# First convolution by halves of the images, its norm finished in two parts, parameters prepared beside it

## The chip, the cores and the metric

The kernel runs on one core of one Trainium2 chip. The time is that of the whole program on the device, in microseconds (us); lower is better. TensorE is called PE, VectorE DVE, ScalarE ACT, GpSimd POOL and SyncE SP, as in the profile.

## The reference

Two layers work on 32 images of 96 channels, 56 x 56 points, all in float32:

```python
# layer 0
h = conv7x7_per_channel(x) + conv_b
h = (h - mean_over_channels(h)) * rsqrt(var_over_channels(h) + 1e-5) * ln_g + ln_b
h = gelu(h @ w1 + b1)          # 96 -> 384, at each point
h = (h @ w2 + b2) * layer_scale
x = h + x
# layer 1
x = silu(conv5x5_per_channel(x) + conv_b)
dts, Bs, Cs = split(x_proj_w @ x)
delta = softplus(dt_w @ dts + dt_b)
P = exp(cumsum(max(delta * A, log(1e-9))))
hs = P * cumsum(delta * Bs * x / max(P, 1e-9))
y = sum_n(hs * Cs) + x * Ds
```

The mean and the variance at a point go over all 96 channels, so the first convolution must be done for every channel before a point can be normalised.

## The kernel before

The program has four stages, each with its own pools in SBUF: the first convolution, the MLP, the second convolution, and the scan. Between them everything goes through DRAM.

**Preparation.** SP loads all parameters (L105 to L131) and then the two sets of convolution kernels. DVE spreads the 7 x 7 kernels into zeroed rows (`pad`, L150 to L156), SP stores them as `taps1_d`, and from there they come back as Toeplitz matrices. In between stand the 5 x 5 kernels (`taps2_d`) and the MLP's and the scan's weights: folded with the norm's gain and the layer scale by small matmuls (L182, L190, L207) and copied into place by DVE.

**First convolution.** The 32 images lie as two halves of 16 (`j`), 56 image rows each, so 112 rows of 896 points for a channel. For each of the 96 channels SP loads the Toeplitz matrix `wt` (two DMAs from `taps1_d`, in `toeplitz`, three buffers) and the two image halves `xt`; DVE, POOL and ACT copy even and odd columns into `xq` (three zeroed buffers); PE does four taps by two halves (L286), both with the same weights one after the other; ACT adds the bias into `ht` (L294); POOL's queue stores `ht` to `conv1_d` (L298). DVE and ACT keep running sums of the difference to channel 0 and of its square (`acc1`, `acc2`, L302 to L305). After the last channel the norm is finished for all points (L308 to L316): square, subtract, Sqrt on ACT, reciprocal on DVE, and a store to `rstd_d`.

**MLP.** 28 groups of four rows. `load_rows(n)` loads `r` (the norm, repeated over 32 partitions), three tiles `h` of `conv1_d` and three tiles `x` of four DMAs each, two groups ahead. `normalise` multiplies `h` by `r` on DVE; `hidden` does the first matmul (L372, PSUM tiles `ph`, three buffers) and Gelu on ACT (L382); `result` the second (L391, `po`) and the sum with `x` into `o` (L402); POOL's queue stores `o` to `block_d`. A group has two parts `k`, each of three steps in which PE does `hidden` and then `result` of the part before. Groups 0 to 13 hold the rows of half `j = 0`, groups 14 to 27 those of `j = 1`.

**Order.** Instructions marked `pin` keep the order of the text on their engine. The others, those of the first convolution and all loads of the MLP among them, are placed by the compiler's scheduler, which may move them far ahead if buffers and data allow. A DMA on SP's or ACT's queue also waits for one of eight semaphore lanes, that is for the DMA that had this lane before it. Tiles in DRAM are followed by region: a load waits for the stores that write what it reads.

Of the kernel before, what the change touches and what calls it, by code (L numbers as in the profile page):

```python
# [8 lines left out]
F32 = mybir.dt.float32  # L9
# [37 lines left out]
def convnext_then_scan_kernel(  # L47
# [38 lines left out]
    def column(src, n, name):  # L86
        t = const.tile([n, 1], F32, name=name)
        nc.sync.dma_start(t, src.rearrange("(p o) -> p o", o=1))
        return t

    def across(src, parts, n, name):
        t = const.tile([parts, n], F32, name=name)
        nc.sync.dma_start(t, src.rearrange("(o n) -> o n", o=1).to_broadcast([parts, n]))
        return t
# [9 lines left out]

    c1b_t = across(c1b, ROWS, C, "c1b_t")  # L105
    c2b_t = across(c2b, 128, C, "c2b_t")
    g_t = column(ln_g, C, "g_t")
    lnb_t = column(ln_b, C, "lnb_t")
    b2_t = column(b2, C, "b2_t")
    ls_t = column(ls, C, "ls_t")  # L110
    ls_b = across(ls, 128, C, "ls_b")
    dtb_t = column(dtb, C, "dtb_t")
    ds_t = column(ds, C, "ds_t")
    w1_t = const.tile([C, F], F32, name="w1_t")
    nc.sync.dma_start(w1_t, w1)
    b1_t = const.tile([128, 3], F32, name="b1_t")
    nc.sync.dma_start(b1_t, b1.rearrange("(f p) -> p f", p=128))
    w2_t = const.tile([128, 3, C], F32, name="w2_t")
    nc.sync.dma_start(w2_t, w2.rearrange("(f p) c -> p f c", p=128))
    xp_t = const.tile([R, C], F32, name="xp_t")  # L120
    nc.sync.dma_start(xp_t, xp[:R, :])
    xpT_t = const.tile([C, R + 2 * N], F32, name="xpT_t")
    nc.sync.dma_start(xpT_t, xpT)
    dtwT_t = const.tile([R, C], F32, name="dtwT_t")
    nc.sync.dma_start(dtwT_t, dtwT)
    a_t = const.tile([128, NG], F32, name="a_t")
    for g in range(NG):
        nc.sync.dma_start(
            a_t[:, g : g + 1],
            bass.AP(alog.tensor, alog.offset + g * DG, [[1, DG], [C, N], [1, 1]]),  # L130
        )  # L131

    w1r_t = const.tile([128, C // CB, F], F32, name="w1r_t")
    b1p_t = const.tile([128, 3], F32, name="b1p_t")
    b2r_t = const.tile([128, C // CB], F32, name="b2r_t")
    wd_t = const.tile([C, C], F32, name="wd_t")
# [4 lines left out]

    with tc.tile_pool(name="prep", bufs=1) as prep, tc.tile_pool(
        name="prep_ps", bufs=1, space=PSUM
    ) as prep_ps:


        kt = prep.tile([C, K1, K1], F32, name="kt1")
        nc.sync.dma_start(kt, c1w.rearrange("c (i j) -> c i j", j=K1))
        pad = prep.tile([C, 3, WP, P1], F32, name="pad1")
        nc.vector.memset(pad, 0.0)  # L150
        at = H - 1 - K1 // 2
        for i in range(3):
            for t in range(P1):
                j = 2 * t + 1 - i
                if j in range(K1):
                    nc.vector.tensor_copy(pad[:, i, at : at + K1, t], kt[:, :, j])  # L156
        nc.sync.dma_start(taps1_d, pad.rearrange("c d p t -> c (d p t)"))

        kt = prep.tile([C, K2, K2], F32, name="kt2")
        nc.sync.dma_start(kt, c2w.rearrange("c (i j) -> c i j", j=K2))  # L160
        turned = prep.tile([C, K2, K2], F32, name="turned")
        for r in range(K2):
            nc.vector.tensor_copy(turned[:, r], kt[:, K2 - 1 - r])
        pad = prep.tile([C, QC, 2 * RW, QC * 2], F32, name="pad2")
        nc.vector.memset(pad, 0.0)
        for k in range(QC):
            for f in range(QC):
                for t in range(2):
                    j = 4 * t + (k if k < 2 else k - 4) - f + K2 // 2
                    if j in range(K2):  # L170
                        nc.vector.tensor_copy(
                            pad[:, k, RW - K2 : RW, f * 2 + t], turned[:, :, j]
                        )
        nc.sync.dma_start(taps2_d, pad)


        cen = prep.tile([C, C], F32, name="cen")
        nc.vector.tensor_scalar(cen, ident[:C, :C], -1.0 / C, None, ALU.add)
        w1g = prep.tile([C, F], F32, name="w1g")
        nc.vector.tensor_scalar(w1g, w1_t, g_t, None, ALU.mult)  # L180
        ps = prep_ps.tile([C, 512], F32, name="ps_w1")
        nc.tensor.matmul(ps[:, :F], lhsT=cen, rhs=w1g, start=True, stop=True)  # L182
        for i in range(RB):
            for d in range(C // CB):
                nc.vector.tensor_copy(
                    w1r_t[CB * i : CB * i + CB, d, :], ps[CB * d : CB * d + CB, :F]
                )
        ps = prep_ps.tile([128, 512], F32, name="ps_b1")
        for f in range(3):
            nc.tensor.matmul(  # L190
                ps[:, f : f + 1], lhsT=w1_t[:, f * 128 : (f + 1) * 128], rhs=lnb_t,
                start=True, stop=True,
            )
        nc.vector.tensor_add(b1p_t, ps[:, :3], b1_t)

        for f in range(3):
            nc.vector.tensor_mul(w2_t[:, f, :], w2_t[:, f, :], ls_b)
        b2p_t = prep.tile([C, 1], F32, name="b2p_t")
        nc.vector.tensor_mul(b2p_t, b2_t, ls_t)
        for i in range(RB):  # L200
            for d in range(C // CB):
                nc.vector.tensor_copy(
                    b2r_t[CB * i : CB * i + CB, d : d + 1], b2p_t[CB * d : CB * d + CB]
                )

        ps = prep_ps.tile([C, 512], F32, name="ps_wd")
        nc.tensor.matmul(ps[:, :C], lhsT=xp_t, rhs=dtwT_t, start=True, stop=True)  # L207
        nc.vector.tensor_copy(wd_t, ps[:, :C])


        nc.vector.memset(bcw_t, 0.0)
        nc.vector.tensor_copy(bcw_t[:, : 2 * N], xpT_t[:, R:])
        nc.vector.memset(pick_t, 0.0)
        for k in range(4):
            rows = slice(32 * k, 32 * k + 2 * N)
            at = 32 * k + (k // 2) * N
            nc.vector.tensor_copy(
                pick_t[rows].rearrange("p (d n) -> p d n", n=N),
                ident[rows, at : at + N].rearrange("p (o n) -> p o n", o=1).to_broadcast(
                    [2 * N, DG, N]  # L220
                ),
            )
        nc.vector.tensor_reduce(
            sel_t, ident.rearrange("p (d n) -> p d n", n=N), mybir.AxisListType.X, ALU.add
        )
        nc.vector.tensor_scalar(dsm_t, ident[:C, :C], ds_t, None, ALU.mult)
        nc.scalar.activation(a_t, a_t, AF.Exp)
        nc.vector.tensor_scalar(a_t, a_t, -1.0, None, ALU.mult)

    def toeplitz(taps_d, wt, k, c, m):

        n = (k + 1) // 2
        for s in range(2):
            taps = bass.AP(
                taps_d.tensor, taps_d.offset + (c * 3 + 1 - s) * WP * n,
                [[n, H], [WP * n, 2], [1, m * n]],  # L240
            )
            nc.sync.dma_start(wt[MP * s : MP * s + H], taps)
        return wt.rearrange("p o m -> p (o m)").rearrange("p (q t) -> p t q", t=n)
# [4 lines left out]
    def two(t):  # L248
        return t.rearrange("p (s q) -> p s q", s=2)

    with tc.tile_pool(name="c1", bufs=3) as pool, tc.tile_pool(
        name="c1k", bufs=1
    ) as keep, tc.tile_pool(name="c1_ps", bufs=4, space=PSUM) as psum:
        wts = [keep.tile([128, 2, H * P1], F32, name=f"wt1_{i}") for i in range(3)]
        xqs = [keep.tile([128, B2, BI, W2 + 3], F32, name=f"xq_{i}") for i in range(3)]
        for t in wts + xqs:
            nc.vector.memset(t, 0.0)
        first = keep.tile([ROWS, COLS], F32, name="first")
        acc1 = keep.tile([ROWS, COLS], F32, name="acc1")
        acc2 = keep.tile([ROWS, COLS], F32, name="acc2")  # L260
        nc.vector.memset(acc1, 0.0)
        nc.vector.memset(acc2, 0.0)

        def by_row(d, s):

            return d[:, s * PQ : (s + 1) * PQ].rearrange("(j m) q -> m j q", j=B2)

        for c in range(C):
            wv = toeplitz(taps1_d, wts[c % 3], K1, c, H)
            xt = pool.tile([128, COLS], F32, name=f"xt1_{c}", tag="xt")  # L270
            for j in range(B2):
                nc.sync.dma_start(xt[MP * j : MP * j + H], x[c, j * H : (j + 1) * H])
# [24 lines left out]
            for s in range(2):  # L297
                nc.gpsimd.dma_start(by_row(conv1_d[c], s), two(ht)[s * H : (s + 1) * H])  # L298
# [502 lines left out]
```

## Time and profile before

| | |
|---|---|
| time, median of 3 runs | 3668.39 us (3664.61 to 3669.38) |
| profiled execution: time, span | 3661.97 us, 3660.2 us |
| first matmul of the first convolution | 27.68 us |
| one channel of it, steady | 6.03 us |
| ACT takes up its last channel | 608.99 us |
| first matmul of the MLP | 642.85 us |
| first matmul of the second convolution | 1505.63 us |
| PE, DVE, ACT, POOL busy | 83%, 73%, 64%, 53% |
| DMA share, 100 to 500 us and 640 to 1500 us | mostly 0.4 to 0.6 |

The page's slices are 91.5 us each: the first convolution fills slices 1 to 7, the MLP 8 to 16, the second convolution about 17 to 20, the scan the rest. A digit is the busy share in tenths. In a timeline line the first two numbers are start and length, and the bracket gives the idle time before it and what ended that. A group's line has busy time and mean of one in ns, and after the last bar the idle time before its instructions.

### The profile page before, as it was taken

The numbers are of one execution on the slowest core, as the hardware profiler recorded it, in microseconds if no ns is written. First come the engines' busy times: TensorE is split into PE (matmuls) and PEld (weight loads), VectorE is DVE, ScalarE is ACT, GpSimd is POOL, SyncE is SP. The second block draws the span as 40 slices with busy tenths as digits, with TensorE's granted clock in tenths as the row PEclk, the third lists the DMA queues.
The fourth block names the chain that finished last, engine by engine and source line by source line (L and its number), as shares of the span: only waits on it lengthen the run. The fifth ranks groups of instructions, "written<-read, shape, count | busy, mean of one in ns | idle before, by whom it ended". The sixth has DMA issues, their size and how long they took to land. (4 is left out here: it accounts for less than half of the span.)

```text
span 3660.2 us, 46554 instructions
## 1 busy us (share of the span) xinstructions
PE 3054.0 (83%) x17290; PEld 1284.6 (35%) x17290; DVE 2670.0 (73%) x1867; ACT 2343.2 (64%) x2133; POOL 1951.4 (53%) x1241
## 2 busy tenths in 40 slices
PE   7999996899999999899948777777777777777775
PEld 5777774333333333334312222222222222222221
DVE  5666665233333333699949999999999999999998
ACT  3555553333333333588858888888888888888884
POOL 2333331122222222100038998898898898898896
PEclk9999998899999999999966666667667667667666
DMA  5555553455555554699977877877877877877873
GB/s 153 167 167 169 168 166 108 150 162 162 160 163 160 162 158 121 183 285 292 289 235 251 276 245 272 275 258 262 272 250 266 277 256 262 278 253 265 278 256 109
DMA packets 302055, 790.70 MB, mean 216 GB/s; under 512 B 123012, under 2 KB 180164, under 8 KB 277156
## 3 DMA queue, kind: packets, MB, share of 16 engines
q1 hardware_dynamic: 259076, 669.31, 56.6%
q0 software_dynamic: 28416, 79.87, 7.2%
q10 hardware_dynamic: 14336, 38.54, 2.8%
q8 instruction: 137, 2.24, 0.3%
q14 instruction: 90, 0.74, 0.1%
HBM read 551.83 MB, written 235.74 MB: 215 GB/s over the span
## 5 line engine op out<-in xcount | busy, mean ns | idle before, releaser
L681 POOL TENSOR_TENSOR hs<-hs,ct 128x1568 f32<-128x1568 f32 x192 | 672.9, 3505 | 102.8 <-DVE hs L670 91.0
L654 POOL TENSOR_TENSOR rep<-rep,bt 128x1568 f32<-128x1568 f32 x192 | 674.5, 3513 | 14.5 <-DMA rep<-du_d 14.5
L382 ACT ACTIVATE g<-ph,b1p_t 128x896 f32<-128x896 f32 x336 | 320.1, 1004 | 512.2 <-PE ph L372 512.2
L402 DVE SCALAR_TENSOR_TENSOR o<-po,b2r_t,x 128x224 f32<-128x224 f32 x336 | 190.5, 609 | 572.3 <-PE po L391 572.3
L286 PE MATMUL ps<-xq,wt 120*112 120x448 f32 x1536 | 581.2, 539 | 14.4 <-POOL xq L281 14.4
L414 POOL DMA_DIRECT2D block_d<-o x336 | 183.0, 552 | 703.8 <-DVE o L402 621.8
L286 PEld LDWEIGHTS ps<-xq,wt 120*112 120x112 f32 x1536 | 429.4, 280 | 165.9 <-POOL xq L281 14.6
L372 PE MATMUL ph<-h,w1r_t 32*128 32x448 f32 x4032 | 440.1, 559 | 55.7 <-DVE h L362 54.0
L599 POOL TENSOR_TENSOR du<-du,xs 96x784 f32<-96x784 f32 x128 | 236.2, 1846 | 367.1 <-ACT du L593 367.1
L585 PE MATMUL pz<-xs,wd_t 96*96 96x392 f32 x512 | 268.6, 688 | 182.6 <-ACT du L593 147.9
L391 PE MATMUL po<-g,w_t 128*32 128x448 f32 x4032 | 413.1, 543 | 0.0
L694 PE MATMUL py<-hs,sel_t 128*32 128x392 f32 x1536 | 330.0, 680 | 85.5 <-POOL hs L681 85.5
L661 DVE TENSOR_TENSOR_SCAN pv<-rep,pv 128x1568 f32<-128x1568 f32 x96 | 329.1, 3428 | 59.9 <-DMA rep<-du_d 43.3
L666 DVE SCALAR_TENSOR_TENSOR pv<-pv,rep 128x1568 f32<-128x1568 f32 x192 | 345.6, 1800 | 21.1 <-POOL hs L681 1.4
L630 PE MATMUL pk<-bn,pick_t 8*128 8x392 f32 x1024 | 284.9, 672 | 87.2 <-ACT y L704 68.1
L661 DVE TENSOR_TENSOR_SCAN pv<-rep,carry_p,pv 128x1568 f32<-128x1568 f32 x96 | 334.9, 3489 | 9.5 <-DVE hs L670 0.5
L670 DVE TENSOR_TENSOR_SCAN hs<-rep,carry_h,pv 128x1568 f32<-128x1568 f32 x96 | 334.1, 3480 | 10.0
L480 PE MATMUL ps<-xq,wt 128*32 128x448 f32 x3072 | 308.4, 547 | 34.2 <-DMA xq<-block_d 31.8
L670 DVE TENSOR_TENSOR_SCAN hs<-rep,pv 128x1568 f32<-128x1568 f32 x96 | 328.4, 3420 | 9.9 <-PE pk L630 0.5
L503 DVE COPY st<-yt 28x896 f32<-28x896 f32 x288 | 317.6, 1103 | 20.6 <-ACT yt L494 8.5
L687 PE MATMUL py<-xs,dsm_t 96*96 96x392 f32 x512 | 318.9, 768 | 14.5 <-ACT bn L618 9.5
L648 ACT ACTIVATE rep<-rep,a_t 128x1568 f32<-128x1568 f32 x192 | 308.4, 1606 | 12.5 <-DMA rep<-du_d 12.2
(87 smaller groups left out, 3473.1 us busy)
## 6 DMA issues: line engine op xcount, KB each, us to landing
rep<-du_d SPq DMA_DIRECT2D x192, 1568.0 KB
du_d<-du SPq DMA_DIRECT2D x128, 588.0 KB
xq<-block_d SPq DMA_DIRECT2D x192, 225.0 KB
block_d<-o POOLq DMA_DIRECT2D x336, 120.0 KB, 5.6
xt<-in_x_dram SPq DMA_DIRECT2D x192, 196.0 KB
h<-conv_d SPq DMA_DIRECT2D x84, 448.0 KB
x<-in_x_dram SPq DMA_DIRECT2D x336, 112.0 KB
conv_d<-st SPq DMA_DIRECT2D x96, 392.0 KB
```

The costliest lines, as they stand in the source:

```text
L286: nc.tensor.matmul(ps[:, j, :PQ].rearrange("p (i r) -> p i r", i=BI), lhsT=wv[:KR, t], rhs=xq[:KR, j, :, t : t + W2], start=(t == 0), stop ...
L372: pin(nc.tensor.matmul(phs[i // 2][:, i % 2, :HALF], lhsT=w1r_t[rows, d, f * 128 : (f + 1) * 128], rhs=hts[n, d][rows, s * HALF : (s + 1) ...
L382: nc.scalar.activation(gt, ph[:, :, :HALF], AF.Gelu, bias=b1p_t[:, f : f + 1], scale=1.0)
L391: pin(nc.tensor.matmul(po[CB * i : CB * i + CB, :HALF], lhsT=w2_t[:, f, CB * d : CB * d + CB], rhs=gts[n, s, f, i // 2][:, i % 2], start=( ...
L503: pin(copy(st[:, :, :, :, f], yt[RW * f : RW * f + QR].rearrange("p h (b q) -> p h b q", q=QW),))
L654: pin(nc.gpsimd.tensor_mul(ut, ut, bts[i // NG]))
L661: pin(nc.vector.tensor_tensor_scan(run, da, zero, carry_p[:, col : col + 1] if q else 1.0 / EPS, ALU.mult, ALU.add))
L666: pin(nc.vector.scalar_tensor_tensor(run, in0=run, scalar=1.0, in1=ut, op0=ALU.min, op1=ALU.mult))
L670: pin(nc.vector.tensor_tensor_scan(ht, da, run, carry_h[:, col : col + 1] if q else 0.0, ALU.mult, ALU.add))
L681: pin(nc.gpsimd.tensor_mul(ht, ht, cts[k]))
L687: pin(nc.tensor.matmul(half(py[:C], s), lhsT=dsm_t, rhs=tokens(k, 2 * h + s, 4), start=True, stop=False,))
L694: pin(nc.tensor.matmul(py[g * DG : (g + 1) * DG, s, :BK], lhsT=sel_t, rhs=hss[k * NG + g][:, cols], start=False, stop=True, tile_position= ...
```

## The change

The convolution's loop goes over 192 halves `n` instead of 96 channels: first all channels of `j = 0`, then all of `j = 1`, so the taps of a channel are loaded twice. The sums are kept for each half apart. `finish_norm(0)` stands two halves into the second 96, `finish_norm(1)` in the MLP at `k == 3`. The convolution's pools stay open through the MLP, which gets fewer buffers for `x` and `g`. SP loads the 7 x 7 kernels and three image halves first; the other parameters go on ACT's queue, and what prepares them is split into pieces (`beside`) of which one follows each half from the seventh on. Some memsets move from DVE to POOL.

```diff
+    def finish_norm(j):
+        acc1, acc2 = acc1s[j], acc2s[j]
+        sq = keep.tile([ROWS, HALF], F32, name=f"sq_{j}")
+        nc.vector.tensor_mul(sq, acc1, acc1)
...
+        nc.scalar.activation(acc2, acc2, AF.Sqrt, bias=eps_t[:ROWS], scale=1.0)
+        nc.vector.reciprocal(acc1, acc2)
+        for s in range(2):
+            nc.gpsimd.dma_start(
+                rstd_d[j * H : (j + 1) * H, s * PQ : (s + 1) * PQ], acc1[s * H : (s + 1) * H]
+            )
...
+        name="c1_ps", bufs=8, space=PSUM
...
+        kt1 = prep.tile([C, K1, K1], F32, name="kt1")
+        nc.sync.dma_start(kt1, c1w.rearrange("c (i j) -> c i j", j=K1))
+        def load_x(n):
+            j, c = divmod(n, C)
+            xts[n] = pool.tile([H, COLS], F32, name=f"xt1_{n}", tag="xt", bufs=4)
+            nc.sync.dma_start(xts[n], x[c, j * H : (j + 1) * H])
+        for n in range(3):
+            load_x(n)
...
+            nc.scalar.dma_start(t, src.rearrange("(p o) -> p o", o=1))
...
+        beside = [first_weights] + [lambda i=i: first_rows(i) for i in range(RB)]
+        beside += [second_weights, scan_weights, scan_rows, turn_taps]
+        beside += [lambda k=k: second_taps(k) for k in range(QC)]
+        def taps_of(n):
+            c, wt = n % C, wts[n % len(wts)]
+            for s in range(2):
...
+                nc.sync.dma_start(wt[MP * s : MP * s + H], taps)
+        for n in range(2):
+            taps_of(n)
+        for n in range(B2 * C):
+            j, c = divmod(n, C)
+            if n + 2 < B2 * C:
+                taps_of(n + 2)
+            if n + 3 < B2 * C:
+                load_x(n + 3)
+            xq = xqs[n % len(xqs)]
+            xv = xts.pop(n).rearrange("p (i r s) -> p s i r", i=BI, s=2)
+            copy = nc.vector.tensor_copy if n % 2 else nc.gpsimd.tensor_copy
+            copy(xq[:H, :, 2 : W2 + 2], xv[:, 1])
+            nc.scalar.copy(xq[MP:KR, :, 1 : W2 + 1], xv[:, 0])
...
+            for t in range(P1):
+                nc.tensor.matmul(ps..., lhsT=wv[:KR, t], rhs=xq[:KR, :, t : t + W2], ...)
...
+            if n >= 6 and beside:
+                beside.pop(0)()
+            if n == C + 2:
+                finish_norm(0)
...
-            nc.vector.memset(t, 0.0)
+            nc.gpsimd.memset(t, 0.0)
...
-                xt = pool.tile([128, COLS], F32, name=f"x_{n}_{d}", tag="x", bufs=9)
+                xt = pool.tile([128, COLS], F32, name=f"x_{n}_{d}", tag="x", bufs=6)
...
-                gt = pool.tile(..., name=f"g_{n}_{s}_{f}_{a}", tag="g", bufs=15)
+                gt = pool.tile(..., name=f"g_{n}_{s}_{f}_{a}", tag="g", bufs=14)
...
+            if k == 3:
+                finish_norm(1)
```

The buffers: `wt` three, for two halves ahead and the one in use; `xq` four; `xt` four; PSUM eight single banks. As the scheduler has built it, SP's queue in the convolution holds for each half two tap loads and one image load, and between them the MLP's first loads: 24 DMAs of `x` (groups 0 and 1), `h` of group 0 behind the taps of halves 35, 71 and 101, `r` of groups 0 and 1 behind those of 107 and 112, `h` of group 1 behind 117, 122 and 127, `r` of group 2 behind 183, and `h` of group 2 behind 187 (one) and 188 (two). The store of `taps2_d` stands near the tenth half. On DVE the three `normalise` of group 0 come right behind the last addition to `acc2` of `j = 1`, ahead of the second norm's last steps, and on ACT the second Sqrt is the last instruction before Gelu's table.

## The prediction

> **What bounds the kernel now.** I read the page first: slices, then groups. TensorE (PE) is full in slices 2 to 6 and 9 to 16, the two stages that the change touches; from slice 17 on VectorE (DVE) is full, and nothing there is touched.
>
> ```profile
> PE   7999996899999999899948777777777777777775
> PEclk9999998899999999999966666667667667667666
> L286 PE MATMUL ps<-xq,wt 120*112 120x448 f32 x1536 | 581.2, 539 | 14.4 <-POOL xq L281 14.4
> L372 PE MATMUL ph<-h,w1r_t 32*128 32x448 f32 x4032 | 440.1, 559 | 55.7 <-DVE h L362 54.0
> ```
>
> The convolution's group (L286) waited once, 14.4 us, at its start; its steady part is matmul time alone. The next stage's first matmuls (L372) waited 54.0 us for `h`. So there are two holes, at the start and at the join, and the timeline of each shows what ends last.
>
> ```profile
> 10.23 0.59 SPq L148 DMA_DIRECT2D kt<-in_c1w_dram  x1
> ...
> 16.60 0.32 SPq L157 DMA_DIRECT2D taps_d<-pad  x1
> ...
> 20.26 2.32 SPq L242 DMA_DIRECT2D wt<-taps_d  x3
> ...
> 27.68 112.68 PE L286 MATMUL ps<-xq,wt 120*112 120x448 f32 x293 [14.39 <-POOL xq L281]
> ...
> 35.99 1.01 ACT L294 ACTIVATE first<-ps,c1b_t 112x896 f32<-112x896 f32 x1 [3.23 <-PE ps L286]
> ...
> 42.02 1.01 ACT L294 ACTIVATE ht<-ps,c1b_t 112x896 f32<-112x896 f32 x1
> ```
>
> The first kernel taps are asked for only at 10.23, behind all other parameters; their way through DRAM and the image behind them put the first matmul at 27.68. Channel 0 takes 8.3 us, every later one 6.03 (42.02 - 35.99), so the array starts 2.3 us slow.
>
> ```profile
> 608.99 1.01 ACT L294 ACTIVATE ht<-ps,c1b_t 112x896 f32<-112x896 f32 x1 [1.73 <-PE ps L286]
> ...
> 618.65 5.75 DVE L314 RECIPROCAL acc<-acc 112x896 f32<-112x896 f32 x1 [2.45 <-ACT acc L313]
> 624.43 0.75 SPq L316 DMA_DIRECT2D rstd_d<-acc  x2
> ...
> 641.55 1.09 DVE L362 TENSOR_TENSOR h<-h,r 128x896 f32<-128x896 f32 x1 [7.76 <-DMA h<-conv_d]
> ...
> 642.85 1.88 PE L372 MATMUL ph<-h,w1r_t 32*128 32x448 f32 x8 [33.95 <-DVE h L362]
> ...
> 654.03 1.28 ACT L382 ACT_TABLE_LOAD   x1 [35.42 <-PE ph L372]
> ...
> 666.25 2.46 PE L391 MATMUL po<-g,w_t 128*32 128x448 f32 x24
> ```
>
> After the last channel (608.9) come statistics, store, reload of `r`, loads of `h` one after another, the Gelu table and slow first matmuls. The stage is in step when the first `po` starts, at 666.25: 57.3 us after the last convolution matmul.
>
> **The change, part by part.** The sum is made against the profiled execution (span 3660.2, time 3661.97, 6.4 below the median 3668.39).
>
> *Start.* In the changed kernel as built, the taps and three image halves are SP's first loads, and the rest goes on ACT's queue. SP reaches `kt1` at 0.75 instead of 10.23, the ten copies (0.83 us) end near 4.5, the store of the taps is issued near 4.8 (it also waits for the second image), and its way to the reload took 3.66 us before (16.60 to 20.26): taps are loaded from 8.4 and landed near 10.8. ACT is later: 19 issues at about 0.45 us, of which the last three wait for a semaphore lane that the tap store holds, so until 10.3, then the table load (1.28) and its image copy (0.60): first matmul at 12.3. **-15.4**, bounds -13 and -17. The array starts slow either way.
>
> *Preparation inside the convolution.* DVE's copies, the memsets moved to POOL and the loads are hidden: a half lasts 3.015 us on PE, in which DVE has some 2.1 us (three 448-wide operations at about 0.6, by 1.09 for 896; half of a 0.39 copy), ACT 1.7, POOL 1.6. The images are copied three halves ahead, so a DVE or POOL that is late by under 9 us costs nothing. Only the small matmuls lie on the path: their groups were busy 1.60 + 1.44 + 0.63 = 3.7 us in the slow start; warm, half. **+2.5**, bounds 1.2 and 3.7.
>
> *Halves.* The same 768 matmuls at 0.754 us, so no change, if their operands come in time. Taps are now loaded for each half: 200 KB more a channel, and a pair is issued only when the half three back is done, so it must land within two halves, 6.03 us. The windows (last columns: granted clock, DMA share, GB/s) show such a pair:
>
> ```profile
> 205.28:205.78 0.50, 0.50 (x2) 0.32 (x2) 0.00 (x0) 0.50 (x1) 0.00 (x0) 1.00 0.03 2
> 205.78:206.28 0.50, 0.50 (x3) 0.40 (x2) 0.34 (x1) 0.47 (x2) 0.07 (x1) 1.00 0.58 151
> 206.28:206.78 0.50, 0.50 (x3) 0.40 (x2) 0.50 (x1) 0.27 (x1) 0.50 (x1) 1.00 0.67 176
> 206.78:207.28 0.50, 0.50 (x2) 0.32 (x2) 0.47 (x2) 0.00 (x0) 0.50 (x2) 1.00 0.23 74
> ...
> 630.00:636.00 6.00, 0.00 (x0) 0.00 (x0) 3.35 (x4) 0.00 (x0) 0.00 (x0) 0.50 0.26 99
> ```
>
> Issued at 204.85, its bytes flow until about 207.2: 2.35 us of the 6.03. They took 0.5 x (0.58 + 0.67 + 0.23) = 0.74 us of all DMA engines, once more in each 6.03 us, so the convolution's 0.54 becomes 0.66. Room is left: **0**.
>
> *Loads moved into the convolution.* This is what the two holes are paid with. Twelve loads of `r` and `h` (448 KB) now stand in SP's queue between the tap pairs. The last row above shows what one is: 0.26 of the DMA engines at 99 GB/s, so 4.6 us each; the three `h` of before are used 4.7 us apart, and SP's first load behind them was held 4.19 us. Taps behind such a load are late by something between 0 and its whole length. Worst case for a single one, counted from the end of half m-3: pair until 2.3, image 3.1, heavy load 7.8, stores between 8.3, next pair 9.2, needed at 9.05. The first of them also waits on SP for the store of channel 31 (3.9 us from issue to landing), with the taps of half 36 queued behind it: 1 us more at most. So nine single loads cost 0 to 1 us each: **+5** (0 to 10). But near the end `h` of group 2 comes as one load behind the taps of half 187 and two at once behind those of 188. By the same count the first ends at 7.5, taps 188 at 8.4 (needed at 9.05), the two at 18, taps 189 at 19, needed at 12.06: 7 us late, and a slow restart. **+8**, bounds 0 and 11; I take nearly the whole since the row shows such loads keeping others waiting. [...]
>
> *Join.* `r` and `h` of groups 0 and 1 are in SBUF when the last half ends (T). DVE still has subtract, add, square and add for the last channel (four of about 0.6 from T+0.7), then normalise at T+3.1; the first matmul at T+4.3 and the third `h` at T+6.4; then two short operations, the Sqrt on ACT at T+7.5 (its table is still loaded), Gelu's table 8.1 to 9.4, first Gelu done at T+10.3. Before, from there (656.3) to the first `po` were 10.0 us with the same three PSUM buffers: T+20.3 instead of T+57.3. **-37**, bounds -33 and -41 (no slow clock, less waiting for PSUM). In the rows of 612 to 640 the granted clock is 0.50, and it is 1.00 only from 660. [...]
>
> *Afterwards.* The second norm's reciprocal (2.9 us) lies on DVE ahead of the first `po` and is done at T+11. `x` has 6 buffers for 9: loads of group n+2 wait for the results of group n and are needed 44 us later; 12 of them took SP 23 us. **0**. POOL's store of a norm waits for the reciprocal with the stores of later halves behind it; nobody reads those for many halves. The next stage's memsets and loads still wait for the last stores of `block_d`: **0**.
>
> Sum: -15.4 + 2.5 + 5 + 8 - 37 = -36.9. The profiled span would be near 3623; from the median 3668.4 the time is **3631.5**.
>
> **The rivals.**
> (a) The moved loads keep no taps waiting: -15.4 + 2 - 37 = -50, 3618. For it: the other three quarters of the engines were free. Against it: SP held for 4.19 us.
> (b) Each single load holds taps for 2.5 us and the group at the end 11: -15.4 + 2.5 + 22.5 + 11 - 37 = -16, 3652.
> (c) Slower: the halved lead of the taps sets the pace. It decides from 0.19 us a half (36.9 / 192), that is when a pair needs over 6.4 us to land. With 7 us the half is 3.5 us: +93, in all +56, 3725. For it: three streams in one queue and no spare buffer; against: 2.35 us measured, and 34% of the DMA time free.
> (d) The MLP stage becomes paced by `x` with six buffers; 2 us in each of 26 groups would be +52, 3683. Against: 20 us of slack.
> That the first norm isn't finished beside the convolution after all is excluded by the built order: the loads of `r` for groups 0 and 1 stand behind the taps of halves 107 and 112.
>
> **How the numbers follow.** My sum 0.57, (a) 0.20, (b) 0.12, (c) 0.07, (d) 0.04. All low bounds together give -17 + 1.2 - 41 = -57 (3611), all high ones -13 + 3.7 + 10 + 11 - 33 = -21 (3647); to hold (b) too, 3652. A difference under 0.2% (7 us) can't be told from none: faster 0.89 (the first three), same 0.02, slower 0.09.
>
> **What would show it.** Right: first L326 near 12, 3.015 us a half, pauses of PE at the late halves, above all one of some 7 us near half 189, first `po` some 20 us after the last convolution matmul, the later stages unchanged. Wrong: PE waiting for taps in every half (c), DVE waiting for `x` (d), no pause at 189 (a), or a start that ACT's queue puts after 15.

## The result: slower by 1%, and the profile after

The changed kernel takes 3702.9 us (median of 5 runs, 3697.3 to 3703.9) against 3666.4 for the kernel before, 1.0096 times as long (95% interval 1.0084 to 1.0107). The forecast was 3631.5 and faster. The profiled execution has a span of 3700.7 us, 40.5 more than before.

The page's slices, now of 92.5 us, and two groups:

```profile
PE   7999799899999999899957777777777777778775
PEclk9999999999999999999976666666666666666666
L326 PE MATMUL ps<-xq,wt 120*112 120x448 f32 x1536 | 606.8, 556 | 74.1 <-DMA wt<-taps_d 48.6
L406 PE MATMUL ph<-h,w1r_t 32*128 32x448 f32 x4032 | 436.0, 556 | 21.7 <-DVE h L396 19.3
```

The join did what was forecast: L406 waits 19.3 us for `h` instead of 54.0. But the convolution's group, which had waited only at its start, now waits 74.1 us, 48.6 of them put down to the taps, and its matmuls are busy for 25.6 us more at the same count, which the granted clock below explains. TensorE's own timeline shows where:

```profile
62.31 69.70 PE L326 MATMUL ps<-xq,wt 120*112 120x448 f32 x184
137.28 111.86 PE L326 MATMUL ps<-xq,wt 120*112 120x448 f32 x288 [5.26 <-DMA wt<-taps_d]
254.24 93.32 PE L326 MATMUL ps<-xq,wt 120*112 120x448 f32 x240 [5.10 <-DMA wt<-taps_d]
353.28 20.94 PE L326 MATMUL ps<-xq,wt 120*112 120x448 f32 x48 [5.72 <-DMA wt<-taps_d]
377.02 15.40 PE L326 MATMUL ps<-xq,wt 120*112 120x448 f32 x40 [2.81 <-ACT dt L345]
395.86 17.10 PE L326 MATMUL ps<-xq,wt 120*112 120x448 f32 x40 [3.42 <-DVE acc L346]
...
465.05 172.11 PE L326 MATMUL ps<-xq,wt 120*112 120x448 f32 x448 [7.52 <-DMA wt<-taps_d]
641.95 13.93 PE L326 MATMUL ps<-xq,wt 120*112 120x448 f32 x32 [4.79 <-DMA wt<-taps_d]
657.10 3.35 PE L326 MATMUL ps<-xq,wt 120*112 120x448 f32 x8 [1.22 <-DMA wt<-taps_d]
670.08 12.21 PE L326 MATMUL ps<-xq,wt 120*112 120x448 f32 x24 [9.63 <-DMA wt<-taps_d]
686.80 4.67 PE L406 MATMUL ph<-h,w1r_t 32*128 32x448 f32 x28 [4.51 <-DVE h L396]
```

Eight records are one half. Each of these pauses follows one of the loads of `r` and `h`, and between 465 and 637, where none stands, there is none. Two of them, behind the loads of `r` issued at 367.02 and 385.15, are put down to ACT and DVE; when the loads are moved away (e1 below) these two are gone like the rest. The stretch after a pause is mostly too long as well: 288 records are 36 halves, 108.5 us at 3.015, and took 111.86. So the first load cost 5.26 + 3.3 us. (Behind the pause of 2.81 us the clock stayed at 1.00, and 40 records took 15.40 us, where five halves are 15.08.) The timeline around the first load:

```profile
125.02 0.66 SPq L384 DMA_DIRECT2D h<-conv_d  x1
...
126.02 0.76 SPq L307 DMA_DIRECT2D wt<-taps_d  x2
...
129.03 1.07 SPq L307 DMA_DIRECT2D wt<-taps_d  x2
...
132.05 4.71 SPq L307 DMA_DIRECT2D wt<-taps_d  x2
...
137.28 5.56 PE L326 MATMUL ps<-xq,wt 120*112 120x448 f32 x7 [5.26 <-DMA wt<-taps_d]
```

The pair that TensorE wants at 132.0 was issued on time, at 126.02, right behind the load, and is usable only at 137.28, 11.3 us later; a pair had 6.03. The next thing to see is 132.05: of two issues that need 0.75 us together, the second hangs until 136.4, for the semaphore lane that the load holds. So the load itself lasted from 125.0 to 136.4, 11.4 us and not the 4.6 of my sum; read in the same way, the eight loads up to 465 us lasted 9.4 to 12.3. The windows (the last columns are granted clock, DMA share, GB/s) say why:

```profile
101.00:125.00 24.00, 24.00 (x65) 17.83 (x64) 16.18 (x28) 14.56 (x24) 10.98 (x20) 1.00 0.71 205
134.00:135.00 1.00, 0.00 (x0) 0.00 (x0) 0.30 (x2) 0.58 (x1) 0.06 (x1) 1.00 0.71 246
135.00:136.00 1.00, 0.00 (x0) 0.00 (x0) 0.38 (x1) 0.00 (x0) 0.00 (x0) 1.00 0.29 109
136.00:137.00 1.00, 0.00 (x0) 0.00 (x0) 0.00 (x0) 0.00 (x0) 0.00 (x0) 0.85 0.27 101
137.00:138.00 1.00, 0.72 (x1) 0.48 (x2) 0.00 (x0) 0.00 (x0) 0.00 (x0) 0.50 0.58 174
```

Before the load the DMA engines are already 0.71 busy. From 135 on, when most else has stopped and TensorE still waits for taps, the share is 0.27 to 0.29 at about 100 GB/s, near the 0.26 of a load alone (though POOL's stores are 0.17 of the 0.29 and 0.05 of the 0.27). Most of the engines are idle then, so it isn't the total bandwidth that the taps lack. At 137 the clock is 0.50.

The end of the convolution and the start of the array:

```profile
682.38 0.63 ACT L334 ACTIVATE ht<-ps,c1b_t 112x448 f32<-112x448 f32 x1 [0.40 <-PE ps L326]
...
701.46 2.46 PE L425 MATMUL po<-g,w_t 128*32 128x448 f32 x24
```

```profile
12.88 1.94 ACTq L201 DMA_DIRECT2D a_t<-in_alog_dram  x3
13.21 3.23 SPq L307 DMA_DIRECT2D wt<-taps_d  x6
...
14.86 0.60 ACTq L206 DMA_DIRECT2D kt<-in_c2w_dram  x1
...
15.49 1.28 ACT L322 ACT_TABLE_LOAD   x1 [15.49 <-DMA a_t<-in_alog_dram]
...
16.79 2.06 ACT L322 COPY xq<-xt 56x448 f32<-56x448 f32 x4
...
17.47 3.31 PE L326 MATMUL ps<-xq,wt 120*112 120x448 f32 x4 [17.47 <-ACT xq L322]
```

From the last convolution matmul (682.3) to the first `po` are 19.2 us. The start came at 17.47: ACT's parameter loads reach to 15.5 and its table load and image copy stand behind them, and SP gets to the taps only at 13.21.

### The profile page after: what moved, and what is told of

Its sections match the earlier page's. It is cut to its first block, busy times and chain, and to the rows that moved or that the text cites. A ratio compares the mean times of both kernels' runs of the same rounds, so it can differ in the third digit from the quotient of the medians.

```text
span 3700.7 us, 47792 instructions
## 1 busy us (share of the span) xinstructions
PE 3084.0 (83%) x17290; PEld 1284.7 (35%) x17290; DVE 2700.3 (73%) x2150; ACT 2387.1 (65%) x2325; POOL 2046.5 (55%) x1446
## 5 line engine op out<-in xcount | busy, mean ns | idle before, releaser
L326 PE MATMUL ps<-xq,wt 120*112 120x448 f32 x1536 | 606.8, 556 | 74.1 <-DMA wt<-taps_d 48.6
L406 PE MATMUL ph<-h,w1r_t 32*128 32x448 f32 x4032 | 436.0, 556 | 21.7 <-DVE h L396 19.3
L623 PE MATMUL pz<-xs,wd_t 96*96 96x392 f32 x512 | 281.1, 715 | 164.5 <-ACT du L631 128.7
L708 DVE TENSOR_TENSOR_SCAN hs<-rep,carry_h,pv 128x1568 f32<-128x1568 f32 x96 | 334.0, 3479 | 10.1
L541 DVE COPY st<-yt 28x896 f32<-28x896 f32 x288 | 317.0, 1101 | 24.6 <-DMA conv_d<-st 9.8
L336 POOL DMA_DIRECT2D conv_d<-ht x380 | 196.3, 521 | 241.3 <-ACT ht L334 224.3
```

The costliest lines, as they stand in the source:

```text
L326: nc.tensor.matmul(ps.rearrange("p (i r) -> p i r", i=BI), lhsT=wv[:KR, t], rhs=xq[:KR, :, t : t + W2], start=(t == 0), stop=(t == P1 - 1),)
L406: pin(nc.tensor.matmul(phs[i // 2][:, i % 2, :HALF], lhsT=w1r_t[rows, d, f * 128 : (f + 1) * 128], rhs=hts[n, d][rows, s * HALF : (s + 1) ...
L541: pin(copy(st[:, :, :, :, f], yt[RW * f : RW * f + QR].rearrange("p h (b q) -> p h b q", q=QW),))
L708: pin(nc.vector.tensor_tensor_scan(ht, da, run, carry_h[:, col : col + 1] if q else 0.0, ALU.mult, ALU.add))
```

## The experiments

The letters are those of the expectations. My theory after the trace (A): a load of `r` or `h` fills its four DMA engines (0.26 of the sixteen where it ran alone, in the kernel before) for some 12 us, because the convolution's own traffic needs them too; the taps behind it land late, and the array restarts slow. Against it stand: taps, loaded twice, that are too many anyway (B); late operands from the preparation (C); the order of SP's queue (D, A1); the lane that holds SP (E).

The stages, worked out from each kernel's TensorE timeline, in us: the first matmul of the convolution, from it to the end of its last, and from there to the first `po`. From the first `po` to the last, the MLP takes 828.5 to 828.7 in all of them; from the second convolution's first matmul to the end are 2152.4 to 2160.1. Each ratio is taken against the kernel before as it ran beside that kernel (medians 3665.2 to 3666.5).

| kernel | median | ratio to before (95%) | first matmul | convolution | join |
|---|---|---|---|---|---|
| before | 3666.4 | 1 | 27.68 | 581.2 | 57.4 |
| changed | 3702.9 | 1.0084 to 1.0107 | 17.47 | 664.8 | 19.2 |
| e1_after_taps | 3631.7 | 0.9896 to 0.9925 | 16.98 | 588.1 | 31.1 |
| e2_split | 3624.6 | 0.9878 to 0.9908 | 17.01 | 587.8 | 20.6 |
| e3_act_queue | 3673.7 | 1.0015 to 1.0039 | 17.88 | 638.7 | 20.1 |
| e4_lead | 3632.6 | 0.9890 to 0.9923 | 16.80 | 598.2 | 20.6 |
| e5_split_late_params | 3614.4 | 0.9844 to 0.9873 | 11.78 | 584.5 | 21.2 |
| e6_before_split | 3653.8 | 0.9957 to 0.9980 | 27.94 | 581.9 | 43.2 |
| e7_three_whole | 3645.0 | 0.9928 to 0.9957 | 16.73 | 614.5 | 20.1 |
| e8_columns | 3627.3 | 0.9878 to 0.9907 | 17.01 | 590.5 | 20.7 |
| e9_lead_too | 3616.8 | 0.9846 to 0.9879 | 11.46 | 585.8 | 20.1 |

**e1: the loads behind the last taps.**

```diff
-                nc.sync.dma_start(wt[MP * s : MP * s + H], taps)
+                pin(nc.sync.dma_start(wt[MP * s : MP * s + H], taps))
...
-                nc.sync.dma_start(ht, rows_of(conv1_d, row, d))
+                pin(nc.sync.dma_start(ht, rows_of(conv1_d, row, d)))
```

(the same `pin` around the load of `r`)

> The changed kernel, but all loads of r and h are held in SP's queue behind the last taps, so none stands inside the convolution (the 24 small loads of x still do). Theory A (a load of r or h keeps four DMA engines for some 12 us, the taps behind it land late and PE restarts slow: about 7 us for each of the twelve): no pause for taps, the convolution from its first to its last matmul takes 583 us instead of 665, the join grows from 19 to about 25 us, total near 3627. Rival B (the taps, loaded twice, and the images fill the queues whatever else is loaded): pauses remain, the convolution stays above 650, total 3700 to 3710. Rival C (the preparation and the first norm on DVE, ACT and POOL make operands late): the pauses near halves 6 to 18 and 98 remain, some 20 us, total 3640 to 3650.

Measured: 3631.7, the convolution 588.1 and the join 31.1, some 5 and 6 us above what was expected. B falls: the same taps twice and the same images, and not one pause for taps.

```profile
L326 PE MATMUL ps<-xq,wt 120*112 120x448 f32 x1536 | 584.9, 542 | 18.8 <-ACT xq L322 17.0 <-ACT dt L345 1.8
```

What idles is the start and one pause of 1.8 us; that is all the waiting there is of C. The twelve loads moved into the convolution thus cost 664.8 - 588.1 = 76.7 us and saved 31.1 - 19.2 = 11.9 at the join.

**e2: each load in four pieces of 32 partitions.**

```diff
-                nc.sync.dma_start(ht, rows_of(conv1_d, row, d))
+                for i in range(RB):
+                    nc.sync.dma_start(
+                        ht[CB * i : CB * i + CB], conv1_d[CB * d : CB * d + CB, row + i, :]
+                    )
```

(`r` likewise; the scheduler puts a piece behind about every fifth pair)

> The changed kernel, but each load of r and h is four DMAs of 32 partitions, 112 KB each, as the loads of x are; they stay inside the convolution. Theory A (the load occupies four of the sixteen engines because its slowest dimension is 4): the pieces spread over all engines, pauses under 1 us each, the convolution 583 to 590 us, join at most the 19 us of the changed kernel, total 3620 to 3630. Rival B: the convolution stays above 650, total 3700. Rival D (any further bytes in SP's queue push taps behind, since they go in order): the same bytes cost the same, 60 to 80 us, total 3680 to 3700.

Measured: 3624.6. No pause for taps is left:

```profile
64.77 540.04 PE L326 MATMUL ps<-xq,wt 120*112 120x448 f32 x1432
```

The join is 20.6 us, a little above the 19 expected. D falls: 26 of the pieces stand among the taps in SP's queue and cost no pause. But not all loads stayed inside: the scheduler set the last six pieces of group 1 behind the last taps, and those of group 2 only at the end of the convolution (from 604.95). So this run clears six and a half of the eight single loads (e8 below keeps all eight inside); the group at the end was moved away and is not tested in pieces here.

**e3: the whole loads on ACT's queue.**

```diff
+            queue = nc.scalar if n < 3 else nc.sync
...
-                nc.sync.dma_start(ht, rows_of(conv1_d, row, d))
+                queue.dma_start(ht, rows_of(conv1_d, row, d))
```

> The changed kernel, but r and h of groups 0 to 2 are issued on ACT's queue instead of SP's, whole. They still go to four engines and take a semaphore lane each. Theory A1 (taps stand behind the load in the same queue): with a queue of their own the taps pass, pauses under 2 us, the convolution below 605 us, total 3625 to 3645. Rival A2 (the four engines are simply full for 12 us, whatever the queue): pauses of 3 us or more stay, total 3660 to 3700. Rival E (SP is held because the load's semaphore lane comes round to it, 24.6 us in six waits): the lanes are shared by both queues, so the pauses stay at about their size, total near 3700.

Measured: 3673.7, the convolution 638.7. A1 falls. The first load in the timeline:

```profile
125.63 0.61 ACTq L385 DMA_DIRECT2D h<-conv_d  x1
...
126.92 0.77 SPq L307 DMA_DIRECT2D wt<-taps_d  x2
...
129.94 0.75 SPq L307 DMA_DIRECT2D wt<-taps_d  x2
...
136.56 0.33 SPq L153 DMA_DIRECT2D xt<-in_x_dram  x1
...
137.00 13.32 PE L326 MATMUL ps<-xq,wt 120*112 120x448 f32 x30 [4.08 <-DMA wt<-taps_d]
```

The pair issued at 126.92 on another queue, without delay, lands at 137.0, 10.1 us later (11.3 on the same queue), about when the load does (SP's wait for its lane ends at 136.56). For this pause E is excluded too: the pair was issued before SP waited. What is left is A2, the engines. ACT's queue held only the load then, so its own share can be read: 25.3% of the sixteen engines, that is four, from 128 to 131, but 14.4% from 131 to 136, when taps, images and stores moved too. The load isn't served alone on its engines, and lasts the longer for it. The second load, alone too, is followed by a pause of 4.69 us. But the scheduler set the other ten between 331 and 381 us, where nine pauses stand close together and SP waited for lanes, up to 9.7 us at once: how much of those is E, and how much the crowding, can't be told from this run, and its total says little.

**e4: five tap buffers instead of three, a lead of four halves.**

```diff
-    wts = [... for i in range(3)]
+    wts = [... for i in range(5)]
...
-            if n + 2 < B2 * C:
-                taps_of(n + 2)
+            if n + 4 < B2 * C:
+                taps_of(n + 4)
```

> The changed kernel with five tap buffers instead of three, so that a pair is asked for four halves ahead, 12.06 us instead of 6.03; the loads of r and h stay as they are. Theory A: the pair behind a single load landed 11.2 us after its issue, so the single pauses vanish (some 60 us of 82), and what is left is the group near the end, 5 to 15 us: the convolution 588 to 600, total 3630 to 3645. Rival B (throughput of the queues, not lead): buffers put off the first pauses but the loss stays above 50 us, total 3690 or more.

Measured: 3632.6, the convolution 598.2, within what A expected. The first three loads (issued at 139.6, 230.4 and 324.6) pass without a pause, the five that follow some 16 us apart leave three pauses of 2.8 us together, and SP still waits for lanes (27.0 us for `h`, against 24.6 in the changed kernel), which now costs little, so E isn't the price; the group at the end keeps one of 3.31 us:

```profile
64.77 287.39 PE L326 MATMUL ps<-xq,wt 120*112 120x448 f32 x760
...
610.13 4.85 PE L326 MATMUL ps<-xq,wt 120*112 120x448 f32 x8 [3.31 <-DMA wt<-taps_d]
```

**e5: e2, and the parameters behind the first taps.** All but the first bias are collected and issued in the loop, with the taps pinned as in e1; the prepared pieces follow every second half.

```diff
+            if n >= 2:
+                for _ in range(2):
+                    if waiting:
+                        pin(nc.sync.dma_start(*waiting.pop(0)))
-            if n >= 6 and beside:
+            if n >= 14 and n % 2 == 0 and beside:
                 beside.pop(0)()
```

> The split loads of e2, and the parameters (all but the first bias) are issued on SP behind the first taps, two for each half, instead of on ACT's queue ahead of its first copy; the prepared pieces follow every second half from the fifteenth on. Theory F (the start is late because ACT's 18 parameter loads stand ahead of its table load and copy, and hold semaphore lanes that the taps need): first matmul at 11 to 12.5 instead of 17.0, and the 1.85 us pause of PE near 56 us, where DVE copies weight rows, goes too: total 3614 to 3619. Rival G (the way of the taps through DRAM and the first table load set the start): first matmul at 15.5 to 17, total 3621 to 3625.

Measured: 3614.4, the fastest here. F holds: TensorE starts at 11.78 and its last wait is now for the taps, not for ACT.

```profile
5.67 1.28 ACT L337 ACT_TABLE_LOAD   x1 [5.67 <-DMA xt<-in_x_dram]
...
8.66 2.54 SPq L322 DMA_DIRECT2D wt<-taps_d  x6
...
11.78 4.60 PE L341 MATMUL ps<-xq,wt 120*112 120x448 f32 x7 [11.78 <-DMA wt<-taps_d]
```

The pause near 56 is gone as well. A new one of 1.32 us stands at 121, behind the store of the second taps (786 KB, issued at 114.0).

**e6: the pieces alone, in the kernel before.** The edit of e2 in the old kernel.

> The kernel before with the loads of r and h in four pieces each, as in e2. It has none of them inside the convolution, so what it gains shows what the pieces do at the join alone: h of group 0 landed 14 to 23 us after its issue at 628; in pieces over all engines 4 to 10. Theory A: first po 10 to 15 us earlier, total 3650 to 3656, well above the 3624.6 of e2, whose gain then lies in the change and not in the pieces. Rival H (the pieces speed up the MLP itself): total below 3640.

Measured: 3653.8; the join falls from 57.4 to 43.2, the first matmul and the convolution stay within 0.7 us, and the MLP stays at 828.5. H falls: of the 41.7 us by which e2 beats the kernel before, 12.6 are to be had from the pieces without the change.

**e7: three loads whole again.** As e2, with `h` of group 0 in one DMA each.

> As e2, but the three h of group 0 are loaded whole again, alone in the convolution (behind the taps of halves 36, 72 and 102); everything else is in pieces. Theory A: three pauses of about 5 us, each followed by a slow restart of about 3 us: 3 x 8.2 = 24.6 us more than e2, total 3649. Rival I (a single load is harmless, and only loads that follow each other within 50 us hurt): within 5 us of e2, total 3625 to 3630.

Measured: 3645.0 (3642.2 to 3649.9), 20.3 more than e2 by the medians and 27.9 by the profiled spans, against 24.6 expected; the convolution alone is 26.7 longer, 8.9 a load. I falls. Three loads, three pauses:

```profile
137.88 111.35 PE L326 MATMUL ps<-xq,wt 120*112 120x448 f32 x288 [6.46 <-DMA wt<-taps_d]
257.24 93.31 PE L326 MATMUL ps<-xq,wt 120*112 120x448 f32 x240 [8.01 <-DMA wt<-taps_d]
357.81 273.43 PE L326 MATMUL ps<-xq,wt 120*112 120x448 f32 x720 [7.26 <-DMA wt<-taps_d]
```

**e8: four pieces by columns, the 4 rows still outermost.**

```diff
-                nc.sync.dma_start(ht, rows_of(conv1_d, row, d))
+                for i in range(RB):
+                    q = slice(i * COLS // RB, (i + 1) * COLS // RB)
+                    nc.sync.dma_start(ht[:, q], rows_of(conv1_d, row, d)[:, :, q])
```

> The changed kernel with each load of r and h cut in four by columns: 128 partitions x 224, 112 KB each as in e2, but with the 4 rows still outermost, so still on four of the sixteen engines, and placed one or two halves apart. Theory A-size (what counts is how long one load fills its engines): a piece fills them for 3 us instead of 12, the pair behind it lands within its 6.03 us, pauses under 2 us outside the group at the end, total 3625 to 3640. Rival A-engines (four engines are too few in any portion, since pieces one or two halves apart leave them no room: their share is 0.66 without the pieces and 0.2 to 0.4 more with them): pauses in most places where pieces stand, total 3660 to 3700.

Measured: 3627.3, no slower than e2 beyond its scatter (their ranges overlap). In 347 us there is no pause, with pieces one or two halves apart:

```profile
62.64 347.08 PE L326 MATMUL ps<-xq,wt 120*112 120x448 f32 x920
411.00 187.26 PE L326 MATMUL ps<-xq,wt 120*112 120x448 f32 x496 [1.28 <-DMA wt<-taps_d]
```

Two more, of 0.89 and 1.65 us, stand at the end beside the first pieces of group 2. SP waits 0.7 us in all for the lane of a piece of `h` up to 600 us, where the changed kernel waited 24.6 for whole ones. The rival that four engines are too few in any portion falls: the outermost dimension is still 4 (no row shows such a piece alone). What hurts isn't this 4 as such. It is how long one load keeps its engines in one go, against a lead of 6.03 us. How much of that length is due to the four engines isn't tested: no run has a whole load spread over sixteen.

**e9: e5 with the lead of e4.**

> e5 with five tap buffers, so a lead of four halves. What is left of pauses in e5 is one of 1.32 us at 122.6, behind the store of the second taps (786 KB, issued at 114.0), with a slow restart of about 2 us. Theory A (any long transfer is covered by a lead that is longer than it): no pause, the convolution 581 to 582 us instead of 584.5, total 3610 to 3612. Rival: more taps in flight delay the start or the last loads of h, total 3614 or more.

Measured: 3616.8 (3612.8 to 3617.6), no better than e5. The pause at 121 is gone as expected, but two short ones (0.47 and 0.91 us) came before it, whose cause isn't shown, and the convolution is 1.2 us longer. The expected 3610 to 3612 was missed.

## Why the prediction was wrong

By its own steps, in spans: forecast -36.9, measured +40.5, so 77.4 to explain.

- *Start*: -10.2 instead of -15.4 (5.2 of the miss). I gave ACT's queue 0.45 us an issue and a wait only for its last three; in fact it reached 15.5, and SP waited for ACT's lanes too: 3.7 us before its third image load and 4.0 before the taps. e5 shows that the way of the taps was nearly right: without that queue the first matmul waits for the taps alone and starts at 11.78, where I had them landed near 10.8.
- *Preparation* and *halves*: up to the first whole load the convolution lost 6.0 us against 3.015 a half, 2.3 before: +3.7 instead of +2.5. The halved lead alone costs nothing (e1), so rival (c) is out.
- *Loads moved into the convolution*: **this step failed.** The sum had +5 for nine singles and +8 for the end. The eight singles up to 637 us cost 58.9 (505.1 us for 148 halves of 3.015), the last four, the ninth single among them, 21.0 (45.1 us for eight halves): +80 instead of +13, 67 of the 77. Of the 58.9 us, 39.2 are pauses and 19.7 slow matmuls behind them, which the +5 left out. The pause announced near half 189 came, with 9.6 us for the 7. The mechanism was named rightly, "late by something between 0 and its whole length", and the upper end was wrong: the whole length was taken as the 4.6 us of a row in which nothing else moved, and the count "from the end of half m-3" used that. The paragraph before it puts the convolution's own traffic at 0.66 of the DMA time. Both numbers together would have warned: as a rough estimate, 4.6 / (1 - 0.66) = 13.5 us, more than two halves. Measured were 11.4, and a traffic of 0.71; with that the estimate is 15.9, so it is an upper figure.
- Nor was it rival (b): a single load cost 58.9 / 8 = 7.4 us where (b) had 2.5. No rival priced a load beside full traffic: of the two slower ones, (c) looked at the taps alone and (d) at the MLP's `x`.
- *Join*: -38.2 against -37, by the steps given.
- *Afterwards*: the MLP is unchanged (828.6), so rival (d) is out. From the second convolution on the profiled run is 5.2 longer, which lies within the 2152.4 to 2160.1 of kernels that don't touch that part.
- The number of engines: in the kernel before, the loads of `r` and `h`, 4 rows outermost, show 0.25 to 0.26 of the sixteen alone (629.9 to 636 us), and in e3 one of `h` shows 25.3% on a queue of its own. The two stores of `rstd_d` in the kernel before, 56 rows outermost, showed 0.82 together (625.5 to 626.75), and `h` with the `x` pieces of 32 rows beside it 0.86 (636.75 to 639.5). So the share went with the shape, as theory A of e2 has it; that the outermost rows are the reason was my assumption, which no run separates, and that e8's pieces stay on four engines is an estimate from the 0.26. As e8 keeps the outermost 4 and loses almost nothing, this shape alone does not set the price.

That the loads cost so much decides the sign: without them (e1) the change gives 3631.7, by chance the forecast itself; with the loads in pieces (e2) 3624.6.

## What to carry to other kernels

A transfer's length read where it ran alone was a lower bound here: 4.6 us alone, 9.4 to 12.3 beside steady traffic. Dividing by the share that this traffic leaves free gave an upper estimate in this one case; compare it with the lead, in us, of whatever is loaded behind it. A scheduler that hoists the next stage's loads into a tight loop puts them where the lead is shortest: cut them into pieces that fit the lead, or buffer deeper, before counting on hidden loads. A queue of its own for the long load took 1.2 us off the delay of the pair behind it (10.1 for 11.3) and did not remove the pause.

## What the runs showed of the hardware

- The length of a pause alone does not tell whether TensorE restarts slow. The same pause of 1.84 or 1.85 us near 55 us was followed by a granted clock of 0.50 in e1, e2 and e4, and left it at 1.00 in the changed kernel, e3, e7 and e8. In e1 the pause lies at 54.9 to 56.7; the clock steps down some 0.6 us after work has resumed and stays down for some 3.4 us (granted clock third from the end):

```profile
55.00:56.00 1.00, 0.00 (x0) 0.00 (x0) 0.97 (x2) 0.29 (x1) 0.99 (x1) 1.00 0.39 131
...
57.00:58.00 1.00, 1.00 (x3) 0.54 (x3) 1.00 (x4) 0.44 (x1) 0.90 (x2) 0.68 0.58 119
58.00:59.00 1.00, 1.00 (x3) 0.54 (x2) 0.53 (x1) 0.38 (x1) 0.13 (x1) 0.50 0.81 252
```

  In the changed kernel, after the same pause:

```profile
56.00:57.00 1.00, 1.00 (x4) 0.71 (x4) 1.00 (x4) 0.41 (x1) 0.93 (x2) 1.00 0.55 114
57.00:58.00 1.00, 1.00 (x4) 0.81 (x3) 0.49 (x1) 0.41 (x1) 0.11 (x1) 1.00 0.85 245
```

  The pause of 1.32 us in e5 left the clock at 1.00.
- The tap pair on a queue of its own still took 10.1 us beside the load, against 11.3 on the load's queue. The load's share in e3 went down from 25.3% to 14.4% when taps, images and stores moved too; why the pair still landed hardly earlier stays open: no run here separates the order inside an engine from its being full.
